# A state-space scan on one core: one state's input of each chunk made by VectorE in place of GpSimd, its row of B broadcast by TensorE

## The chip, the core and the metric

The kernel runs on one core of a Trainium2 chip. The metric is the device time of one execution in microseconds (us). The engines are called PE (TensorE; PEld is its loading of weights), DVE (VectorE), ACT (ScalarE), POOL (GpSimd) and SP (SyncE, which here issues the DMAs). Each has its own instruction queue, works through it in order, and waits for the others by semaphores.

## The reference, cut to what matters

For each of 8 images (56 x 56 pixels, 192 channels) a first layer normalises, runs separable convolutions and attention, and adds the result. A second layer projects to 384 channels, convolves, and runs a selective scan over the 3136 pixels in four directions, 16 states each:

```python
def step(h, inp):
    u_l, d_l, B_l, C_l = inp
    dA = jnp.exp(d_l[..., None] * A)
    dBu = d_l[..., None] * B_l[:, :, None, :] * u_l[..., None]
    h = dA * h + dBu
    y = jnp.sum(h * C_l[:, :, None, :], axis=-1)
    return (h, y)
```

`d` and `u` have a value for every pixel and channel, `B` and `C` one for every pixel and state. The outputs `y` of the four directions are added, normalised, gated and projected. The change concerns `dBu`: the product of `d*u` (made earlier, `du`) with the row of `B` that belongs to one state.

## The kernel before, in words

The scan works in chunks of T = 448 pixels: 7 chunks by 4 directions by 8 images are 224 chunks, and in each chunk 16 states follow one another. The 384 channels lie as NJ = 3 blocks of 128 partitions. For one state `n` of a chunk this happens:

- `row_loads` (line 1098 on) has SP load the row of `B` from DRAM onto all 128 partitions, the tile `bb` (five buffers; 224 KB written to SBUF).
- `inputs_made` (line 1113 on) takes one of seven buffers `h` and has POOL multiply `du` with `bb` into it, 128 x 1344 elements (line 1119).
- `decays` has ACT make the factors exp(d*A), one block at a time, into one of two PSUM banks `da` (line 1133).
- `scans` has DVE run the recurrence along the pixels, in place in `h`, block by block (line 1150); `carries` keeps the last column (line 1172).
- For most states TensorE transposes `h` in four pieces of 112 pixels into the PSUM tile `ht` (`turned`, line 1196), ACT scales it by `C`, which is then one number for each partition, into `g` (line 1212; the column of `C` comes from `ct_s`), and TensorE transposes it back and adds it up in the PSUM tile `y` (`back`, line 1230).
- For the states named in `BY_POOL` (2 and 6, 9 and 13; in the last image 2 and 7, 12) POOL multiplies `h` with a broadcast row of `C` and adds two such products (lines 1248 and 1252), and TensorE adds the sum to `y` (line 1267).
- At the end of a chunk DVE adds `y` to the image's sum (`evicted`, three instructions of line 1282 or 1284). There is one `y`, in three PSUM banks.

PSUM has eight banks: three for `y`, two for `da`, and three that are shared. Of the shared ones `ht` may hold up to two and the rest of the kernel ("bank1") one at a time.

While the scan of an image runs, the first layer of the next image is woven in: in its first part convolutions (line 452) and attention (lines 756 and 765), then the projections of its scan (`x_proj`, lines 936 to 956, where POOL also makes `du`, line 920). In its last direction the finished image is normalised, gated and written (`finish`, lines 984 to 1036).

The order of all engines' queues is fixed when the program is built. Each step is a generator that yields engine, assumed cost, what it reads and what it writes; a planner (`Sched`) always gives out the step that could start soonest, less a rank in us. `pace` ties the next image's TensorE time to the progress of the scan: 87% of it is spread over the first three directions, the rest over the fourth. Where the planner sees TensorE idle for long, it puts in small products with zeros (`warm`, line 1363), the fills. `share(name, most)` (line 1311 on) makes a user of the three shared banks; a bank is asked for with `yield`, and comes free when the instruction that reads it out is placed.

The columns of `C` come from `ct_out` (line 889 on): the transposed projection is copied by DVE from PSUM, stored to DRAM, and loaded again by `prepared`, a chunk ahead, as `ct_s`.

Of the kernel before, what the change touches and what calls it, by code (L numbers as in the profile page):

```python
# [18 lines left out]
L = HW * HW  # L19
# [20 lines left out]


BY_POOL = (((2, 7), (12,)), ((2, 6), (9, 13)))
EPS = 1e-5
CAP = 60.0
HBUFS = 7
# [228 lines left out]
def kernel(  # L274
# [198 lines left out]
    def front(b):  # L473
# [308 lines left out]
        with tc.tile_pool(name=f"fw_{b}", bufs=1) as fw, tc.tile_pool(name=f"fi_{b}", bufs=2) as pool:  # L782
# [7 lines left out]
            for i, w in enumerate((wx, wz)):  # L790
# [10 lines left out]
                rows=[dbatch.tile([2 * NST, L], F32, name=f"rows{k}") for k in range(NDIR)],  # L801
                dl=[dbatch.tile([128, NJ, L], F32, name=f"dl{k}") for k in range(NDIR)],
                du=[dbatch.tile([128, NJ, L], F32, name=f"du{k}") for k in range(NDIR)],
                ct=[dbatch.tile([TP, L // TP, NST], F32, name=f"ct{k}") for k in range(NDIR)],
                k_rows={}, k_ct={}, k_dl={}, k_du={})

            tiles, ends = {}, []
# [67 lines left out]
    def x_proj(b, todo):  # L875
# [3 lines left out]
        with tc.tile_pool(name=f"p2_{b}_{todo[0][1]}", bufs=2) as pool:  # L879
# [7 lines left out]
                    inputs[lay, c] = xs  # L887

            def ct_out(pct, lay, c):
                ct = yield p2("ct", [TP, 2, SUB, NST])  # L890
                yield DVE, 0.25, pct.c, ct.c
                nc.vector.tensor_copy(ct.ap, pct.ap[:TP, :].rearrange("p (s k r) -> p k s r", k=2, r=64)[:, :, :, R + NST:NR])
                pct.free()
                for i in range(2):
                    k = lay + 2 * i
                    m["k_ct"][k, c] = Cell()
                    yield from dma(ct.c, [m["k_ct"][k, c]], 2.9, m["ct"][k][:, c * SUB:(c + 1) * SUB], ct.ap[:, i])
                ct.free()
# [150 lines left out]
    for b in range(nb):  # L1049

        for k in (0, 1, 3, 2):
            order = range(NCH) if k < 2 else range(NCH - 1, -1, -1)
            steps += [(b, k, c, i) for i, c in enumerate(order)]
    todo = [(i, n) for i in range(len(steps)) for n in range(NST)]
    by = [BY_POOL[b < nb - 1] for b, *_ in steps]
    by = [{n: (n == g[0], n == g[-1]) for g in groups for n in g} for groups in by]

# [13 lines left out]
    def prepared():  # L1071

        for i, (b, k, c, _) in enumerate(steps):
            yield lambda: b in made and all((k, c) in made[b][s] for s in ("k_ct", "k_rows", "k_dl", "k_du"))
            m = made[b]
            cols = slice(c * T, (c + 1) * T)
            du = yield s2("du_s", [128, NJ, T])
            yield from dma([m["k_du"][k, c]], du.c, 5.5, du.ap, m["du"][k][:, :, cols])
            dl = yield s2("dl_s", [128, NJ, T])
            yield from dma([m["k_dl"][k, c]], dl.c, 5.5, dl.ap, m["dl"][k][:, :, cols])  # L1080
            ct = yield s2("ct_s", [TP, SUB, NST])
            yield from dma([m["k_ct"][k, c]], ct.c, 1.8, ct.ap, m["ct"][k][:, c * SUB:(c + 1) * SUB])
            chunks[i] = (dl, du, ct)

# [13 lines left out]
    def row_loads():  # L1098
        for i, n in todo:
            b, k, c, _ = steps[i]  # L1100
            yield lambda: i in chunks
            m = made[b]
            cols = slice(c * T, (c + 1) * T)
            bb = yield s3("bb", [128, T], 5)
            yield from dma([m["k_rows"][k, c]], bb.c, 3.2, bb.ap, m["rows"][k][n, cols].partition_broadcast(128))
            brow[i, n] = bb
            if n in by[i]:
                cbr = yield s2("cb", [128, T])
                yield from dma([m["k_rows"][k, c]], cbr.c, 3.2, cbr.ap,
                               m["rows"][k][NST + n, cols].partition_broadcast(128))  # L1110
                crow[i, n] = cbr

    def inputs_made():
        for i, n in todo:
            yield lambda: (i, n) in brow
            bb, du = brow.pop((i, n)), chunks[i][1]
            h = yield sh("h", [128, NJ, T], parts=2 + NJ)
            yield POOL, t_pool(NJ * T), bb.c + du.c, [h.c[0]]
            nc.gpsimd.tensor_tensor(h.ap, du.ap, bb.ap.unsqueeze(1).to_broadcast([128, NJ, T]), ALU.mult)  # L1119
            bb.free()  # L1120
            if n == NST - 1:
                du.free()
            states[i, n] = [h, 2]

    def decays():
        for i, n in todo:
# [75 lines left out]
    def scaled():  # L1202
        for i, n in todo:
            if n in by[i]:
                continue
            for s in range(SUB):
                yield lambda: (i, n, s) in turns
                ct = chunks[i][2]
                ht = turns.pop((i, n, s))
                g = yield s3("g", [TP, DIN])  # L1210
                yield ACT, 0.47, ht.c + ct.c, g.c
                nc.scalar.activation(g.ap, ht.ap[:TP, :DIN], AF.Copy, scale=ct.ap[:, s, n:n + 1])  # L1212
                ht.free()
                gs[i, n, s] = g
            if n == NST - 1:
                ct.free()
# [72 lines left out]
    with tc.manual_schedule():  # L1289
# [11 lines left out]
        with ExitStack() as es:  # L1301
            py = es.enter_context(tc.tile_pool(name="py", bufs=1, space=PSUM))
            pa = es.enter_context(tc.tile_pool(name="pa", bufs=2, space=PSUM))
            pb = [es.enter_context(tc.tile_pool(name=f"pb{i}", bufs=1, space=PSUM)) for i in range(3)]
            ybanks = py.tile([128, NJ, 512], F32, name="y")
            nc.vector.memset(ybanks, 0.0)
            ry = Ring(lambda: ybanks, 1)
            rda = Ring(lambda: pa.tile([128, 512], F32, name="da"), 2)
            three = [Tile(1) for _ in pb]

            def share(name, most):
                return Share(three, [lambda p=p: p.tile([128, 512], F32, name=name, tag="bank") for p in pb], most)

            rht = share("ht", 2)
            banks[0] = share("bank1", 1)
            at["chunk"] = 0
            for g, rank in ((prepared, 0.3), (skips, 0.0), (row_loads, 0.25), (inputs_made, 0.0), (decays, 0.37),
                            (scans, 0.16), (carries, 0.36), (turned, 0.37), (scaled, 0.38), (by_pool, 0.39),
                            (back, 0.4), (summed, 0.0), (evicted, 0.71)):
                sc.spawn(g(), rank, "scan")  # L1320

            per = NDIR * NCH * NST

            def ended(b):
                first = b * NDIR * NCH + (NDIR - 1) * NCH
                yield lambda: at["chunk"] >= first
                yield from finish(b, lambda c: lambda: at["chunk"] >= first + NCH - c, yread[b])

            def arounds():
                for b in range(nb):  # L1330
                    yread[b] = {}
                    sc.spawn(ended(b), 0.0, "finish")
                    if b > 0:
                        yield lambda: at["chunk"] >= b * NDIR * NCH
                    else:
                        yield from sc.join([sc.spawn(x_proj(0, order[LEAD:]), 0.0, "front")])
                    if b + 1 < nb:
                        yield from sc.join([sc.spawn(front(b + 1), 0.0, "front")])
                        yield from sc.join([sc.spawn(x_proj(b + 1, order), 0.0, "front")])

            def pace():

                b, slot = divmod(at["scan"], per)
                whole = main + len(order) * each
                lead = each * (len(order) - LEAD)
                before = b * whole + (lead if b else 0.0)
                here = whole + (0.0 if b else lead)
                late, share = (NDIR - 1) * NCH * NST, 0.87
                part = share * slot / late if slot < late else share + (1.0 - share) * (slot - late) / (per - 2 * NST - late)
                want = before + here * part  # L1350
                return want + 12.0, want - 12.0

            def ending():
                done = sum(len(r) for r in yread.values())
                b, c = divmod(at["chunk"], NDIR * NCH)
                come = b * NCH + max(c - (NDIR - 1) * NCH, 0)
                return 1e9, 1e9 if done < come - 1 or done < b * NCH else 0.0

            def warm():

                while True:
                    yield PE, T_FILL, [], []
                    nc.tensor.matmul(ybanks[:, 0, T:T + FILL], zeros, zeros[:, :FILL], start=False, stop=False)  # L1363

            def may():
                y = ys.get(at["y"])
                return y is not None and y["left"][0] > 0 and y["on"]

            at["y"] = -1
            filler = Stage(warm(), 0.0, 0.0, None)  # L1370
            sc.resume(filler)
            sc.filler = filler, may
            sc.limit["front"] = pace
            sc.limit["finish"] = ending
            sc.spawn(arounds(), 0.0)
            sc.run()
# [58 lines left out]
```

## Time and profile before

| | us |
|---|---|
| median of three runs | 18205.7 (18203.6 to 18205.72) |
| the profiled execution, its own time | 18215.8 |
| its span, first to last instruction | 18214.1 |
| evictions of the fifth image end | 9741 to 11950 |
| evictions of the last image end | 16366 to 18167 |

The span is cut into stretches in some views. A busy time is the sum over an engine's records in the stretch, with the number of instructions behind it; records of PE, DVE and ACT overlap in part, since an instruction starts while the one before it is still draining. A group's row gives line, engine, operation, what it writes and reads, shapes, number, then busy time and mean ns of one, then the idle time of the engine just before these instructions and what ended most of it. A wait's row says who waited for whom, and gives total us, number of waits and the longest.

The chain of work that ended last is followed in this profile only from 16093 us to the end, so it tells of the last image alone, which the change leaves as it is. The mean granted clock of TensorE is 0.982.

### The profile page before, as it was taken

What the parts mean: (1) busy time and instruction counts of PE and PEld (TensorE: products, weight loads), DVE (VectorE), ACT (ScalarE), POOL (GpSimd) and SP (SyncE); (2) the same over time, 40 slices, a digit from 0 to 9 for tenths busy, and PEclk for the clock granted to TensorE, in tenths of its full rate; (3) what the DMA queues carried; (4) which work ended last, traced back from release to release, by engine and by line L of the source; (5) the groups of instructions that cost most, each with busy time, mean ns of one, the idle gap of its engine ahead of it and who ended that gap; (6) DMA issues with size and microseconds to landing.
All of it is one profiled execution on the core that took longest, in us unless ns stands there. A gap on an engine that the chain in (4) does not pass through costs nothing. (4 is left out here: it accounts for less than half of the span.)

```text
span 18214.1 us, 279960 instructions
## 1 busy us (share of the span) xinstructions
PE 16706.4 (92%) x99872; PEld 11743.7 (64%) x99872; DVE 14151.5 (78%) x17811; ACT 14223.5 (78%) x25030; POOL 15560.9 (85%) x5200
## 2 busy tenths in 40 slices
PE   8799999999999999999999999999999999999998
PEld 4466666666666666666666666666666666667776
DVE  2277777788878788787887877878878788888998
ACT  2377788687877878778787887878888787888888
POOL 0288899888998889888898889988899888999998
PEclk9899999999999999999999999999999999999999
DMA  1353345433453334533344334553345433453332
GB/s 54 115 161 90 94 142 158 119 90 107 140 170 97 94 112 139 163 99 95 116 147 152 99 92 120 150 150 95 96 127 155 135 93 95 135 153 120 97 96 78
DMA packets 1363539, 2158.99 MB, mean 119 GB/s; under 512 B 176112, under 2 KB 1346016, under 8 KB 1359072
## 3 DMA queue, kind: packets, MB, share of 16 engines
q1 hardware_dynamic: 1362144, 2141.09, 39.7%
q8 instruction: 791, 12.96, 0.3%
q14 instruction: 604, 4.95, 0.1%
HBM read 1649.41 MB, written 491.21 MB: 118 GB/s over the span
## 5 line engine op out<-in xcount | busy, mean ns | idle before, releaser
L1150 DVE TENSOR_TENSOR_SCAN h<-da,newc,h 128x448 f32<-128x448 f32 x9216 | 10104.9, 1137 | 1970.7 <-ACT da L1133 1380.5
L1119 POOL TENSOR_TENSOR h<-du_s,bb 128x1344 f32<-128x1344 f32 x3584 | 10825.3, 3053 | 927.5 <-PE ht L1196 816.2
L1133 ACT ACTIVATE da<-dl_s,acoef 128x448 f32<-128x448 f32 x10752 | 6750.8, 638 | 1756.9 <-DVE h L1150 1705.7
L1212 ACT ACTIVATE g<-ht,ct_s 112x384 f32<-112x384 f32 x10864 | 5847.5, 575 | 936.1 <-PE ht L1196 771.3
L1230 PEld LDWEIGHTS y<-ident,g 112*128 112x128 f32 x32592 | 3564.4, 142 | 2902.0 <-ACT g L1212 1954.4
L1230 PE MATMUL y<-ident,g 112*128 112x112 f32 x32592 | 4799.3, 268 | 654.3 <-ACT g L1212 530.1
L1196 PE MATMUL ht<-ident,h 128*112 128x128 f32 x32592 | 4944.2, 276 | 122.5 <-ACT g L1212 46.6
L1196 PEld LDWEIGHTS ht<-ident,h 128*112 128x112 f32 x32592 | 3683.2, 135 | 482.7 <-DVE h L1150 147.3
L1150 DVE TENSOR_TENSOR_SCAN h<-da,h 128x448 f32<-128x448 f32 x1536 | 1607.5, 1078 | 459.6 <-ACT da L1133 410.9
L1248 POOL TENSOR_TENSOR yp<-h,cb 128x1344 f32<-128x1344 f32 x448 | 1366.3, 3050 | 407.6 <-PE y L1267 173.7
L1248 POOL TENSOR_TENSOR h<-h,cb 128x1344 f32<-128x1344 f32 x420 | 1281.6, 3051 | 292.0 <-issue 171.9
L1363 PE MATMUL y<-zeros 128*128 128x64 f32 x11648 | 1486.5, 271 | 0.0
L1363 PEld LDWEIGHTS y<-zeros 128*128 128x128 f32 x11648 | 1444.5, 194 | 50.2 <-issue 50.2
L920 POOL TENSOR_TENSOR v<-v,xs 128x1344 f32<-128x1344 f32 x224 | 677.3, 3043 | 824.7 <-DMA dl<-v 773.6
L1252 POOL TENSOR_TENSOR yp<-yp,h 128x1344 f32<-128x1344 f32 x420 | 1280.1, 3048 | 32.2
L452 PE MATMUL bank<-xa,dg 128*128 128x440 f32 (+2 forms) x3024 | 1237.1, 535 | 24.2 <-ACT xv L824 19.2
L1267 PE MATMUL y<-yp,ident 128*128 128x448 f32 x2688 | 1223.4, 546 | 10.7 <-POOL yp L1252 10.2
L756 PE MATMUL bank<-qT,kT 128*112 128x448 f32 x2352 | 1074.5, 573 | 138.6 <-DVE oT L719 82.9
L765 PE MATMUL bank<-pT,vt 112*128 112x448 f32 x2352 | 999.9, 543 | 12.4 <-ACT g L1212 6.6
L706 ACT ACTIVATE pT<-bank,nsh 112x448 f32<-112x448 f32 x1176 | 740.1, 632 | 207.2 <-PE bank L756 167.1
L452 PE MATMUL bank<-band,dgq 96*96 96x440 f32 (+3 forms) x2016 | 806.4, 532 | 10.7 <-ACT hq L582 7.7
L452 PEld LDWEIGHTS bank<-xa,dg 128*128 128x128 f32 x3024 | 525.8, 191 | 364.6 <-issue 289.9
(146 smaller groups left out, 11082.0 us busy)
## 6 DMA issues: line engine op xcount, KB each, us to landing
bb<-rows SPq DMA_DIRECT2D x3584, 224.0 KB, 3.4
cb<-rows SPq DMA_DIRECT2D x868, 224.0 KB, 3.7
dl<-v SPq DMA_DIRECT2D x224, 672.0 KB, 5.0
du<-v SPq DMA_DIRECT2D x224, 672.0 KB, 6.1
du_s<-du SPq DMA_DIRECT2D x224, 672.0 KB, 4.5
dl_s<-dl SPq DMA_DIRECT2D x224, 672.0 KB, 4.6
xt<-x1d SPq DMA_DIRECT2D x224, 336.0 KB, 4.6
xch<-xv SPq DMA_DIRECT2D x24, 1568.0 KB, 7.3
```

What stands on the lines that cost most here:

```text
L452: nc.tensor.matmul(out[:, o0:o1, a:b], lhs, img(lo, hi)[:, :, a + dx - 1:b + dx - 1], start=(t == TAPS[0]), stop=(t == TAPS[-1]))
L756: nc.tensor.matmul(ps.ap[:TP, :T], kts[h][:, kb * TP:(kb + 1) * TP], qh.ap, start=True, stop=True)
L1119: nc.gpsimd.tensor_tensor(h.ap, du.ap, bb.ap.unsqueeze(1).to_broadcast([128, NJ, T]), ALU.mult)
L1133: nc.scalar.activation(da.ap[:, :T], dl.ap[:, j], AF.Exp, scale=acoef[:, k * NJ + j, n:n + 1])
L1150: nc.vector.tensor_tensor_scan(h.ap[:, j, rev], da.ap[:, 0:T][:, rev], h.ap[:, j, rev], news[i - 1].ap[:, j, n:n + 1] if ci else 0.0, ALU. ...
L1196: nc.tensor.transpose(ht.ap[:TP, j * 128:(j + 1) * 128], h.ap[:, j, s * TP:(s + 1) * TP], ident)
L1212: nc.scalar.activation(g.ap, ht.ap[:TP, :DIN], AF.Copy, scale=ct.ap[:, s, n:n + 1])
L1230: nc.tensor.matmul(y["t"].ap[:, j, s * TP:(s + 1) * TP], g.ap[:, j * 128:(j + 1) * 128], ident[:TP, :TP], is_transpose=True, start=(n == 0 ...
L1248: nc.gpsimd.tensor_tensor(to.ap, h.ap, cbr.ap.unsqueeze(1).to_broadcast([128, NJ, T]), ALU.mult)
L1252: nc.gpsimd.tensor_tensor(yp.ap, yp.ap, h.ap, ALU.add)
L1267: nc.tensor.matmul(y["t"].ap[:, j, :T], ident, yp.ap[:, j], start=False, stop=(y["left"][j] == 0))
L1363: nc.tensor.matmul(ybanks[:, 0, T:T + FILL], zeros, zeros[:, :FILL], start=False, stop=False)
```

## The change

For state 7 of every chunk of the first seven images the load of `bb` and POOL's product go. In their place TensorE transposes the column of `B` of that state, read 128 times over, in four pieces of 112 pixels into one PSUM bank (`bc`): each of the 128 partitions then holds the row. DVE multiplies `du` with it into `h`. For this the columns of `B` have to be in `ct_s` beside those of `C`, so that the tiles and copies of `ct` become twice as wide. `bc` is a further user of the three shared banks and may hold one.

```diff
 BY_POOL = (((2, 7), (12,)), ((2, 6), (9, 13)))
+BY_DVE = ((), (7,))
...
-                ct=[dbatch.tile([TP, L // TP, NST], F32, name=f"ct{k}") for k in range(NDIR)],
+                ct=[dbatch.tile([TP, L // TP, 2 * NST], F32, name=f"ct{k}") for k in range(NDIR)],
...
             def ct_out(pct, lay, c):
-                ct = yield p2("ct", [TP, 2, SUB, NST])
-                yield DVE, 0.25, pct.c, ct.c
-                nc.vector.tensor_copy(ct.ap, pct.ap[:TP, :].rearrange("p (s k r) -> p k s r", k=2, r=64)[:, :, :, R + NST:NR])
+                ct = yield p2("ct", [TP, 2, SUB, 2 * NST])
+                yield DVE, 0.35, pct.c, ct.c
+                nc.vector.tensor_copy(ct.ap, pct.ap[:TP, :].rearrange("p (s k r) -> p k s r", k=2, r=64)[:, :, :, R:NR])
...
+    by_dve = [BY_DVE[b < nb - 1] for b, *_ in steps]
...
-            ct = yield s2("ct_s", [TP, SUB, NST])
+            ct = yield s2("ct_s", [TP, SUB, 2 * NST])
...
-            bb = yield s3("bb", [128, T], 5)
-            yield from dma([m["k_rows"][k, c]], bb.c, 3.2, bb.ap, m["rows"][k][n, cols].partition_broadcast(128))
-            brow[i, n] = bb
+            if n in by_dve[i]:
+                brow[i, n] = None
+            else:
+                bb = yield s3("bb", [128, T], 5)
+                yield from dma([m["k_rows"][k, c]], bb.c, 3.2, bb.ap, m["rows"][k][n, cols].partition_broadcast(128))
+                brow[i, n] = bb
...
             h = yield sh("h", [128, NJ, T], parts=2 + NJ)
+            if n in by_dve[i]:
+                sc.spawn(input_made(i, n, h), 0.1)
+                continue
...
+    def input_made(i, n, h):
+        _, du, ct = chunks[i]
+        bc = yield rbc
+        yield PE, 0.41, ct.c, bc.c
+        for s in range(SUB):
+            nc.tensor.transpose(bc.ap[:, s * TP:(s + 1) * TP], ct.ap[:, s, n:n + 1].to_broadcast([TP, 128]),
+                                ident[:TP, :TP])
+        yield DVE, 1.45, bc.c + du.c, [h.c[0]]
+        nc.vector.tensor_tensor(h.ap, du.ap, bc.ap[:, :T].unsqueeze(1).to_broadcast([128, NJ, T]), ALU.mult)
+        bc.free()
+        states[i, n] = [h, 2]
...
-                nc.scalar.activation(g.ap, ht.ap[:TP, :DIN], AF.Copy, scale=ct.ap[:, s, n:n + 1])
+                nc.scalar.activation(g.ap, ht.ap[:TP, :DIN], AF.Copy, scale=ct.ap[:, s, NST + n:NST + n + 1])
...
-            rht = share("ht", 2)
+            rht, rbc = share("ht", 2), share("bc", 1)
```

`BY_DVE[b < nb - 1]` is `(7,)` for the first seven images and empty for the last one.

## The prediction, made before the changed kernel ran

> **What bounds the kernel now.** I read the engines' busy shares first, then the granted clock, then the stretches of one image, then the waits inside two of them. The page's first line of busy times puts no engine at its limit over the whole span:
>
> ```profile
> PE 16706.4 (92%) x99872; PEld 11743.7 (64%) x99872; DVE 14151.5 (78%) x17811; ACT 14223.5 (78%) x25030; POOL 15560.9 (85%) x5200
> ```
>
> PE's 92% is no 92% of its capacity: the records overlap (a 268 ns record of line 1230 is followed by the next 96 ns later, in the timeline), and 1486 us of it are the fills of line 1363, which stand only where PE would be idle. POOL's records hardly overlap: in the timeline one 3.05 us operation follows another after 3.00 us. So POOL, at 85% in all, is the fullest engine, and the question is where it is full.
>
> I cut the fifth image (9741 to 11950 us) at the ends of its evictions (lines 1282 and 1284, three for each chunk): chunks 1 and 2, 3 to 15, 16 to 20, 21 to 28. The fifth row is from the last image. Columns: stretch, length, busy time and instructions of PE, PEld, DVE, ACT, POOL, granted clock, DMA share, GB/s.
>
> ```profile
> 9741.00:9975.00 234.00, 212.34 (x1286) 155.57 (x1284) 154.42 (x217) 150.03 (x241) 167.76 (x61) 0.96 0.53 167
> 9975.00:10957.00 982.00, 903.81 (x5295) 618.05 (x5295) 809.77 (x1001) 798.65 (x1475) 870.99 (x289) 0.99 0.34 95
> 10957.00:11323.00 366.00, 345.64 (x1965) 236.16 (x1965) 293.67 (x359) 296.14 (x520) 328.35 (x109) 1.00 0.42 121
> 11323.00:11950.00 627.00, 577.77 (x3601) 417.42 (x3601) 511.48 (x645) 526.40 (x878) 600.26 (x201) 0.99 0.50 149
> 16600.00:17600.00 1000.00, 921.54 (x7209) 758.41 (x7208) 913.96 (x1104) 875.94 (x1647) 995.83 (x332) 1.00 0.34 97
> ```
>
> The same stretches for the fills of line 1363 alone (PE and PEld):
>
> ```profile
> 9975.00:10957.00 982.00, 34.17 (x242) 32.44 (x242) 0.99 0.34 95
> ...
> 11323.00:11950.00 627.00, 75.34 (x604) 74.05 (x604) 0.99 0.50 149
> ```
>
> I call the four stretches A, B, C and D. In D POOL is busy 600 of 627 us (96%), PE has 604 fills, and DVE and ACT stand at 82 and 84%: POOL is the limit. In B POOL is at 89% and PE has 242 fills in a stretch half as long again; the next image's attention and convolutions fill PE there. The waits say the same. Columns: total us, times, longest. The first two rows are of B, the other two of D:
>
> ```profile
> POOL h L1119 <- PE ht L1196: 51.9, 22, 5.5
> DVE h L1150 <- POOL h L1119: 19.2, 9, 8.7
> ```
> ```profile
> DVE h L1150 <- POOL h L1119: 8.5, 7, 2.2
> POOL h L1119 <- PE ht L1196: 6.7, 2, 4.1
> ```
>
> In B POOL waits 52 us for TensorE to turn a state and so free one of the seven `h` buffers: POOL is ahead there. In D it almost never waits (6.7 us). C is between (90%); A has 66 us of POOL idle in 234. In the last image POOL is at 99.6%, but there the change moves nothing (`BY_DVE[False]` is empty).
>
> **What is removed.** 7 images x 28 chunks = 196 inputs of state 7 leave POOL, and with them 196 loads of `bb`. Prices, each row with mean ns after the busy time:
>
> ```profile
> L1119 POOL TENSOR_TENSOR h<-du_s,bb 128x1344 f32<-128x1344 f32 x3584 | 10825.3, 3053 | 927.5 <-PE ht L1196 816.2
> ...
> L1230 PEld LDWEIGHTS y<-ident,g 112*128 112x128 f32 x32592 | 3564.4, 142 | 2902.0 <-ACT g L1212 1954.4
> L1230 PE MATMUL y<-ident,g 112*128 112x112 f32 x32592 | 4799.3, 268 | 654.3 <-ACT g L1212 530.1
> ...
> L986 DVE TENSOR_TENSOR yacc<-yacc,bank 128x1344 f32<-128x1344 f32 x56 | 86.3, 1540 | 18.0 <-PE bank L984 18.0
> ```
>
> POOL loses 196 x 3.053 = 598 us, 3.05 a chunk. That is the ceiling of any gain, and it is paid only where POOL is late. The 196 loads cost nothing now but for the 39.3 us that POOL waited for `bb` in all (the wait view of line 1119); 1 of 16 of that is 2 us, which I drop. SP's queue loses the same 196 issues, which wait there for POOL to free a `bb` buffer; what follows them on SP can only come sooner.
>
> **What is added.**
> - TensorE: four transposes a chunk. The nearest row is line 1230, also 112 rows of weights and 112 moving columns, 96 ns from start to start in the timeline; with the gap to other work (four of line 945, 128 columns wide, take 438 ns to the next start) I take 0.43 us. A column read 128 times over as weights stands in no row: if it hides nothing, load and matmul follow one another, 4 x (142 + 268) = 1.64 us; at the least it is free, where a fill gives way. I stay with 0.43, the like row.
> - VectorE: one product of 1344 elements with one operand in PSUM, put on three blocks. Line 986 is that very form: 1540 ns busy, 1.44 us to the next start. Ends: 1.44, and 2.66 us, the pitch where something waited. I take 1.5. Behind it wait the scans of line 1150; for them ACT, which has only two `da` banks, and behind ACT the products `g` and TensorE. In D DVE idles 116 of 627 us, so 8 x 1.5 = 12 us are covered; in B it idles 172 of 982 for 19 us. If that cover fails, it is 1.5 us a chunk.
> - The PSUM bank: `bc` becomes the fourth user of three banks, of which `ht` may hold two and the front one. It is held through 0.43 us of transposes, about one scan in front on DVE (1.1) and the product (1.5): 3.1 us. Meanwhile `ht` or the front has one bank less. With one bank a turn and its scaling follow one another: three transposes (0.33), 0.58 us of ACT and some 0.2 between, 1.1 us, where B has a turn each 1.57 us (982 us by 624 scalings). So it would mostly still keep up. Ends: 0 and the whole hold, 3.1. I take 0.2 a chunk in A, B and C, nothing in D, where the fills show that PE has room.
> - Small things, at nothing: the copy of `ct` doubles from 128 to 256 columns. 286 ns becomes about 416 (by the 609 ns of the 448-column copy at line 591, an estimate), 112 x 0.13 = 15 us of DVE in the whole kernel, under DVE's idle time, 15 us if not. The `ct` DMAs carry twice the bytes, land in a median of 2.1 us, and are a chunk ahead. DVE takes the product in its own queue, so state 7 no longer waits for POOL.
>
> **A rule against it.** The last image is the row: of its 7209 PE instructions in 1000 us all but the 1876 fills and the sums of line 1267 are transposes, and the granted clock is 1.00. The Trainium skill, "TensorE: Matmul & The Clock Gate", Part 4 (PE-mode transpose), holds that transposes do not count for the clock gate as ordinary matmuls do; it also gives a gated clock of half speed. An estimate by that page: 4 x 96 ns would be 0.77 us, 75 us more over 196 chunks if nothing covers it. This case's clock, with 65,000 transposes in it, does not agree, and I leave it out.
>
> **The sum for one image.**
> - A, 2 chunks: POOL's time is worth nothing, PE +0.43, bank +0.2: +1.3 us.
> - B, 13 chunks: the same: 13 x 0.63 = +8.2.
> - C, 5 chunks: 5 x 3.05 = 15.3 us leave POOL, which idles a tenth; I count a third, -5.1, and +3.2 for PE and bank: -1.9.
> - D, 8 chunks: 24.4 us leave POOL, which idles 27; I count eight tenths, -19.5. What is late next is the ring between the `da` exponentials and the scans (waits of 56 and 54 us in D).
>
> Together -11.9 us, times 7 images -83 us (the first image, whose start differs, is taken as the others). The profiled execution took 18215.8 us (span 18214.1), so 18133 for it; the median of the three runs is 10 us lower, 18205.7, which gives **18120 us** (-0.5%). This forecast's own range is 18010 to 18190: D worth five to ten tenths (12 to 24 us), C 0 to 10, PE and bank 4 to 14 us.
>
> **Rivals.**
> - *POOL is the limit in more of the image.* For it: it is the fullest engine in every stretch, and DVE waits for its `h` in all four. Against it: it waits 52 us in B for buffers. Were C and half of B POOL's as well, 8 + 5 + 6 chunks x 3.05 x 0.9 = -52 us, +7 for PE and bank in the rest: -45 an image, 17890.
> - *Nothing changes.* The 3.05 us turn into idle time of POOL in D too, since the scans wait there for `da` (56 us) rather than for POOL (8.5): D and C worth 9 us together, against 9.5 + 3: some +3 an image, 18225. This holds too if the product is put so late on DVE that the scan of state 7 waits as before: the change then doesn't relieve what it means to.
> - *Slower: the bank.* In A, B and C the front holds its one bank nearly always; `bc` leaves `ht` a single one for 3.1 us, three turns lose 0.55 us each (1.1 against ACT's own 0.58), 1.65 us a chunk. 20 x (0.43 + 1.65) = 42 us, less 19.5 in D: +22 an image, +155: 18360. It decides from about 0.8 us a chunk on, where 20 x (0.43 + 0.8) equals the 24.6 us of C and D.
>
> **How the numbers follow.** Chances: the forecast 0.48, POOL further 0.14, nothing 0.16, the bank 0.22. What a measurement of this kernel tells from no change is about 0.2%, 36 us. The forecast lies beyond that but for 0.02: faster 0.60, same 0.18, slower 0.22. Range: from 17950, which leaves out the better part of the first rival, to 18300, which takes in "nothing" and half of the bank.
>
> **What would show it.** In the changed profile line 1119 has 3388 instructions, the new DVE product 196 of about 1.54 us, PE 784 transposes more. D of the fifth image lasts about 608 us, with POOL at 95% or less; B some 990. Waits of `ht` or of the front's bank for the new DVE product, over 0.8 us a chunk, would show the bank rival; POOL waiting more in D by what it lost, with D as long as before, the second; B shorter by 10 us or more, the first. The prediction is wrong above all if B isn't PE's, or if the three banks are the tightest thing in it.

## The result, and the profile after

The changed kernel takes 18455.4 us (median of four runs, 18454.1 to 18460.3) against 18205.7 us of the kernel before, measured beside it: a ratio of 1.0138, 95% interval 1.012 to 1.0155. It is slower by 250 us. The forecast was 18120, and the time lies beyond the upper end of its range, 18300.

The busy line of the page after, for the one shown of before:

```profile
PE 16845.7 (91%) x100648; PEld 11845.6 (64%) x100648; DVE 14427.0 (78%) x18007; ACT 14247.7 (77%) x25030; POOL 14973.1 (81%) x5004
```

The work moved as announced: GpSimd has 196 instructions less, VectorE 196 more, TensorE 776 more (784 transposes, 8 fills less). POOL lost 588 us of busy time, and the kernel became longer. Now the groups of what was moved and added (mean ns of one after the busy time):

```profile
L1127 POOL TENSOR_TENSOR h<-du_s,bb 128x1344 f32<-128x1344 f32 x3388 | 10232.2, 3051 | 919.0 <-PE ht L1216 786.7
...
L1141 DVE TENSOR_TENSOR h<-du_s,bc 128x1344 f32<-128x1344 f32 x196 | 302.8, 1545 | 60.3 <-PE bc L1138 60.3
L1138 PE MATMUL bc<-ident,ct_s 112*128 112x112 f32 x784 | 110.1, 263 | 0.7 <-ACT g L1232 0.2
```

The prices of the single instructions were right: 1545 ns against 1540 for the product, and in the timeline the transposes follow one another every 96 ns. So the loss is not in what the instructions cost but in where they stand. The four stretches of the fifth image in the kernel after, cut at the same evictions as before:

```profile
9860.00:10124.00 264.00, 233.63 (x1377) 169.98 (x1376) 168.53 (x237) 160.67 (x258) 174.54 (x63) 0.95 0.52 163
10124.00:11119.00 995.00, 916.48 (x5314) 626.07 (x5311) 817.46 (x1002) 797.31 (x1470) 825.03 (x274) 0.98 0.33 91
11119.00:11495.00 376.00, 353.31 (x2007) 242.04 (x2008) 308.98 (x374) 301.30 (x528) 318.78 (x106) 1.00 0.37 115
11495.00:12104.00 609.00, 561.28 (x3560) 406.41 (x3558) 512.68 (x636) 515.47 (x860) 564.94 (x189) 1.00 0.48 146
```

A is 264 us in place of 234, B 995 in place of 982, C 376 in place of 366, D 609 in place of 627. D came out as forecast (608), B near it (990); C went the wrong way, and A, where I had counted 1.3 us, took 30 more. The fills in B and D stand nearly as before:

```profile
10124.00:11119.00 995.00, 34.35 (x234) 32.61 (x234) 0.98 0.33 91
...
11495.00:12104.00 609.00, 73.94 (x584) 71.99 (x584) 1.00 0.48 146
```

The waits that were shown for B (two rows) and D (two rows) are now these; POOL waits for buffers as much as before, though it has less to do:

```profile
POOL h L1127 <- PE ht L1216: 59.9, 21, 7.5
...
DVE h L1170 <- POOL h L1127: 14.5, 9, 5.1
```
```profile
POOL h L1127 <- PE ht L1216: 4.5, 2, 2.5
DVE h L1170 <- POOL h L1127: 4.3, 1, 4.3
```

What did grow over the whole span is ScalarE's wait for a turned state, from 771 to 1070 us (before, line 1212; after, line 1232):

```profile
L1212 ACT ACTIVATE g<-ht,ct_s 112x384 f32<-112x384 f32 x10864 | 5847.5, 575 | 936.1 <-PE ht L1196 771.3
```
```profile
L1232 ACT ACTIVATE g<-ht,ct_s 112x384 f32<-112x384 f32 x10864 | 5869.6, 575 | 1279.7 <-PE ht L1216 1070.1
```

The turned states lie in the shared banks, so the bank was the first suspect; the 30 us at the start of each image were the second. The sign that the prediction named for the bank did not come: TensorE and its loads wait some 31.5 us in all for the new product (the view of the tile `bc`, eight rows), 0.16 us a chunk in place of 0.8. The two largest rows:

```profile
PEld ht L1216 <- DVE h L1141: 16.5, 44, 0.8
...
PE ht L1216 <- DVE h L1141: 6.5, 14, 0.6
```

One more view matters for what follows: what TensorE does for the front (the next image's first layer and projections, and the finished image's last steps), which all goes through the tile `bank`. Stretches A and D of the fifth image, before and after (PE, PEld, DVE, ACT, then clock and DMA as above):

```profile
9741.00:9975.00 234.00, 102.73 (x408) 57.17 (x406) 34.10 (x59) 8.85 (x19) 0.96 0.53 167
...
11323.00:11950.00 627.00, 196.28 (x588) 91.74 (x588) 76.90 (x115) 19.81 (x37) 0.99 0.50 149
```
```profile
9860.00:10124.00 264.00, 118.80 (x453) 65.52 (x451) 40.48 (x69) 10.54 (x22) 0.95 0.52 163
...
11495.00:12104.00 609.00, 183.94 (x553) 85.15 (x552) 73.34 (x106) 17.46 (x33) 1.00 0.48 146
```

D has 35 such instructions less after the change, and A 45 more: the two stretches no longer hold the same work.

### The profile page after: what moved, and what is told of

It reads as the page before. It is cut to its first block, busy times and chain, and to the rows that moved or that the text cites. A ratio compares the mean times of both kernels' runs of the same rounds, so it can differ in the third digit from the quotient of the medians.

```text
span 18453.0 us, 280923 instructions
## 1 busy us (share of the span) xinstructions
PE 16845.7 (91%) x100648; PEld 11845.6 (64%) x100648; DVE 14427.0 (78%) x18007; ACT 14247.7 (77%) x25030; POOL 14973.1 (81%) x5004
## 5 line engine op out<-in xcount | busy, mean ns | idle before, releaser
L1127 POOL TENSOR_TENSOR h<-du_s,bb 128x1344 f32<-128x1344 f32 x3388 | 10232.2, 3051 | 919.0 <-PE ht L1216 786.7
```

## The experiments

All times are compared with the kernel before, measured beside them (its median lay between 18207.6 and 18221.8 us). A to D are means over the third to seventh image of the profiled execution, cut at the evictions. "Left over" is the number of pieces of the next image's projections (14 in an image, each begun by one copy `xd` on ScalarE) that start only after the image's last eviction, for these five images.

| kernel | us | minus before | ratio, 95% interval | A | B | C | D | left over |
|---|---|---|---|---|---|---|---|---|
| before | 18205.7 | | | 233 | 982 | 367 | 626 | 3 |
| after | 18455.4 | +250 | 1.0138 (1.012 to 1.0155) | 263 | 997 | 375 | 610 | 4 |
| e1 three directions | 18484.6 | +270 | 1.0143 (1.0128 to 1.0158) | 247 | 1007 | 375 | 623 | 3 |
| e2 last direction | 18325.2 | +110 | 1.0060 (1.0045 to 1.0075) | 260 | 977 | 367 | 620 | 4 |
| e3 row by DMA | 18592.3 | +377 | 1.0205 (1.0188 to 1.0222) | 232 | 997 | 384 | 647 | 2 or 3 |
| e4 no product | 18157.3 | -58 | 0.9967 (0.9954 to 0.998) | 224 | 981 | 366 | 628 | 2 |
| e5 bank alone | 18426.9 | +207 | 1.0113 (1.0098 to 1.0128) | 225 | 1009 | 369 | 632 | 2 |
| e6 VectorE alone | 18326.1 | +106 | 1.0058 (1.0043 to 1.0073) | 230 | 999 | 367 | 627 | 2 or 3 |
| e7 null order | 18216.5 | -4 | 1.0001 (0.9992 to 1.0011) | 236 | 978 | 367 | 629 | 2 |
| e8 after, rank 0.3 | 18452.4 | +232 | 1.0128 (1.0113 to 1.0143) | 264 | 985 | 367 | 627 | 4 |
| e9 TensorE alone | 18124.1 | -98 | 0.9950 (0.9935 to 0.9964) | 243 | 967 | 369 | 616 | 3 |
| e10 bank without TensorE | 18238.6 | +17 | 1.0011 (1.0001 to 1.002) | 247 | 977 | 367 | 614 | 2 or 4 |
| e12 state not turned | 18002.8 | -219 | 0.9879 (0.9863 to 0.9896) | 233 | 966 | 359 | 623 | 2 or 3 |
| e15 last image relieved | 18199.7 | -22 | 0.9989 (0.998 to 0.9999) | 226 | 982 | 368 | 632 | 2 or 3 |
| f1 = e8, pace 0.90 | 18374.3 | +164 | 1.0092 (1.0077 to 1.0107) | 223 | 1014 | 352 | 639 | 1 or 2 |
| f2 = before, pace 0.90 | 18246.3 | +36 | 1.0017 (1.0008 to 1.0027) | 222 | 996 | 349 | 642 | 1 |
| f3 = after, pace 0.90 | 18407.2 | +197 | 1.0110 (1.0095 to 1.0125) | 227 | 1022 | 356 | 634 | 2 |
| f4 = e5, rank 0.3 | 18316.0 | +106 | 1.0059 (1.0044 to 1.0074) | 261 | 980 | 361 | 614 | 4 |
| f5 four states relieved | 18615.7 | +408 | 1.0224 (1.0209 to 1.0239) | 254 | 999 | 364 | 624 | 4 |
| f6 null order 2 | 18199.9 | -8 | 0.9997 (0.9987 to 1.0007) | 232 | 982 | 366 | 626 | 3 |

My theory after the result was "handed back": the gain in D is real, but the start of the next image pays for projections that no longer fit into the shorter D. Its rivals were "bank" (the fourth user of the shared banks), "product" (VectorE's 1.5 us) and "order" (luck of the planner).

### Which directions lose

```diff
-    by_dve = [BY_DVE[b < nb - 1] for b, *_ in steps]
+    by_dve = [BY_DVE[b < nb - 1 and k != 2] for b, k, *_ in steps]
```

> State 7 goes to VectorE only in the first three directions of an image (21 of 28 chunks); the last direction is as before. Theory 'handed back': the changed kernel gains 18 us an image in stretch D and the start of the next image (A) loses 29, because work of the next image's projections is left over when D is shorter. Then here D and A are as before (627 and 234 us), only B and C stay longer (13 + 9 us): about 18205 + 7 x 22 = 18360. Theory 'bank': the fourth user of three banks costs time wherever bc is used, so A stays near 263 us and B and C long: 18205 + 7 x 50 = 18550.

Measured: +270, more than the whole change. D is nearly as before (623), but A is 247, and B 1007. Neither theory had it: A is longer by 14 us although D isn't shorter by much, and it isn't at 263 either.

```diff
-    by_dve = [BY_DVE[b < nb - 1] for b, *_ in steps]
+    by_dve = [BY_DVE[b < nb - 1 and k == 2] for b, k, *_ in steps]
```

> The other half: state 7 goes to VectorE only in the last direction (7 of 28 chunks). 'Handed back': D some 15 us shorter, A of the next image longer by as much or more, 0 to +11 us an image: 18200 to 18290. 'Bank': D shorter, A as before: 18205 - 7 x 15 = 18100.

Measured: +110, above both theories. D gains 6 us and A loses 27, with nothing of the change in A. So A pays for something that is done in D: the part of "handed back" that places the loss stands, though D gained far less than A lost. The two halves together (+380) are more than the whole: the parts don't add.

### The product without the bank

```diff
-        bc = yield rbc
-        yield PE, 0.41, ct.c, bc.c
-        for s in range(SUB):
-            nc.tensor.transpose(...)
         yield DVE, 1.45, bc.c + du.c, [h.c[0]]
-        nc.vector.tensor_tensor(h.ap, du.ap, bc.ap[:, :T]..., ALU.mult)
+        nc.vector.tensor_tensor(h.ap, du.ap, bb.ap..., ALU.mult)
...
```

The row of `B` is loaded into `bb` for state 7 too, as in the kernel before.

> VectorE still makes the product of state 7, but reads the row of B from bb, loaded by DMA as before: no transposes, no bc, no fourth user of the shared banks. 'Bank': B and C lose nothing and A little: 18100 to 18200. 'Product' (the 1.5 us of VectorE in front of the scan of state 7 are what costs, whatever feeds it): as the changed kernel, 18400 to 18460. 'Handed back' alone says nothing of B and C, but keeps A at 250 us or more.

Measured: +377, the slowest but one, and no theory had it. The group's row gives the likely reason; the same product with both operands in SBUF takes 3475 ns in place of 1545:

```profile
L1133 DVE TENSOR_TENSOR h<-du_s,bb 128x1344 f32<-128x1344 f32 x196 | 681.0, 3475 | 1.8 <-PE ht L1208 1.5 <-issue 0.3
```

The 1.93 us more, 196 times, are 378 us, about the loss; how much of them is exposed was not measured, and that the two sums agree so closely is no proof. So this run says nothing of the bank. It is told under the hardware below.

### Relief alone

```diff
-                sc.spawn(input_made(i, n, h), 0.1)
+                h.c[0].w = max(du.c[0].w, h.c[0].r)
+                states[i, n] = [h, 2]
...
+                src = chunks[i][1] if n in by_dve[i] else h
...
                 nc.vector.tensor_tensor_scan(
-                    h.ap[:, j, rev], da.ap[:, 0:T][:, rev], h.ap[:, j, rev],
+                    h.ap[:, j, rev], da.ap[:, 0:T][:, rev], src.ap[:, j, rev],
```

> State 7's input is not made at all in the first seven images: its scan takes du itself (the factor B is left out), so GpSimd is relieved and nothing is put on VectorE, TensorE or the banks. 'Handed back': D about 20 us shorter, A longer by 15 to 25: 18150 to 18250, which would show that relief of GpSimd is worth little in this program whoever does the work. 'Bank' and 'product': nothing is added, so the relief is kept: 18205 - 7 x 20 = 18065 or less.

Measured: -58 us, 0.3 us of each 3.05 us that GpSimd no longer does. This is the run that fells the forecast. D of the fifth image in e4:

```profile
11284.00:11913.00 629.00, 580.07 (x3591) 420.21 (x3591) 510.36 (x640) 527.22 (x875) 574.27 (x191) 0.99 0.49 149
```

POOL is busy 574 us in place of 600 (the 25 us are gone, as worked out), and D is as long as before. POOL was 96% busy there and was not the limit. "Handed back" falls in its first half too: there was no gain in D to hand back.

The same in the last image, where POOL was at 99.6%:

```diff
-BY_DVE = ((), (7,))
+BY_DVE = ((7,), ())
```

> As e4, but the product of state 7 is left out in the last image and made as before in the other seven: 28 chunks in place of 196. There GpSimd is busy 99.6% and waits for nothing, in D of the others 96%. If only the first is a limit: 28 x 2 to 3 us = 56 to 84 us less, 18120 to 18150, as much as e4 gets from 196 chunks. If relief of GpSimd is worth e4's 0.3 us a chunk there too: 18197 or more.

Measured: -22 us. The stretch 16700 to 17600 us of before and of e15:

```profile
16700.00:17600.00 900.00, 830.13 (x6491) 683.05 (x6490) 822.17 (x994) 789.39 (x1484) 895.99 (x299) 1.00 0.34 97
```
```profile
16700.00:17600.00 900.00, 829.63 (x6495) 682.77 (x6493) 822.52 (x994) 790.21 (x1484) 849.13 (x282) 1.00 0.34 93
```

POOL falls from 99.6% to 94%, and the other engines do in these 900 us what they did before, nearly to the instruction (VectorE 994 and 994, ScalarE 1484 and 1484). A chunk takes 60.6 us before and 60.7 in e15, from eviction to eviction. In both kernels the scans of successive states start mostly 3.82 us apart, and 3.32 us apart two states behind those that POOL multiplies. The work of VectorE and of ScalarE comes near to that: three scans of 1.067 us and a carry of 0.08 are 3.28 us; three `da` of 0.56 and four `g` of 0.46 are 3.52 (starts in the timeline). Neither fills 3.82 us alone, and what makes up the rest was not isolated. GpSimd's 20 operations of 3.0 us a chunk need as long, and it works up to seven states ahead: it is always busy, and with one operation less the chunk is no shorter.

### VectorE, TensorE and the bank, one at a time

All four leave the product out like e4, and add one part again.

VectorE's time without bank and TensorE (a sum over `du` whose result isn't used):

```diff
-        nc.vector.tensor_tensor(h.ap, du.ap, bc.ap..., ALU.mult)
+        nc.vector.tensor_reduce(few.ap, du.ap.rearrange("p j t -> p (j t)"), AX.X, ALU.add)
```

> As e4, but VectorE sums du over its 1344 columns (one input, about 1.45 us, the result unused) ahead of the scan of state 7: VectorE's time without transposes and bank. 'Product': 18350 to 18455, 196 x 1.5 = 294 us over e4, every microsecond of it exposed. 'Bank': 18157 to 18220. 'Order': anywhere between.

Measured: +106, so 164 us over e4, of 284 us (196 x 1.45) that were added. It is in B: 999 against 981 us, 1.4 us for each of 13 chunks, nearly the whole 1.45. C and D hide it.

TensorE's transposes into spare columns of `ht`:

```diff
                 for j in range(NJ):
                     nc.tensor.transpose(ht.ap[:TP, j * 128:(j + 1) * 128], ...)
+                if n in by_dve[i]:
+                    nc.tensor.transpose(ht.ap[:, DIN:DIN + TP], <column n of ct, 128 times>, ident[:TP, :TP])
```

> As e4 (no product; state 7 scans du), plus TensorE's four transposes a chunk written to spare columns of the ht tiles that are held anyway: TensorE's 0.4 us a chunk without a bank and without a wait of VectorE. e4 took 18157, e5 (transposes and bank) 18427. 'TensorE's time': 0.4 to 0.5 us x 196 = 80 to 100 us at the most, 18240 to 18260. 'Bank': the rest, so that this run stays at 18157 to 18260, far from 18427.

Measured: -98, 40 us below e4, with more work. TensorE's time costs nothing that can be seen; that the 40 us are the planner's other order is likely, but not shown.

The bank without transposes:

```diff
         bc = yield rbc
-        yield PE, 0.41, ct.c, bc.c
-        <four transposes>
-        yield DVE, 1.45, bc.c + du.c, [h.c[0]]
-        nc.vector.tensor_tensor(h.ap, du.ap, bc.ap..., ALU.mult)
+        yield DVE, 0.08, [], [h.c[0]] + bc.c
+        nc.vector.memset(bc.ap[:, 0:1], 0.0)
```

> As e5, but nothing is transposed: a shared bank is taken for bc, VectorE writes one column of it (0.08 us), the scan waits for that, and the bank is given back. 'Bank': most of the 270 us between e4 and e5 are here, 18300 to 18427, although the hold is short. 'TensorE': near e4, 18157 to 18200. If neither e9 nor this one comes near 18427, it is the joint hold: the bank is kept while the transposes wait for their turn on TensorE.

Measured: +17, 75 us over e4, short of what "bank" expected. B and C are as in e4 or better. The 75 us lie in A, and only in some images: the third and fourth, with 2 pieces left over, have A at 222 us and the D before it at 621; the fifth to seventh, with 4, have 263 and 614. One program shows both, so A follows how much is left over, and not what the program adds to a chunk: A and the D before it together are 844 us with 2 and 877 with 4.

Transposes and bank together, no product:

```diff
-        yield DVE, 1.45, bc.c + du.c, [h.c[0]]
-        nc.vector.tensor_tensor(h.ap, du.ap, bc.ap..., ALU.mult)
+        yield DVE, 0.08, bc.c, [h.c[0]] + few.c
+        nc.vector.tensor_copy(few.ap, bc.ap[:, 0:1])
```

> As e4 (state 7 scans du, no product, B left out there), but the four transposes into bc are made and the scan waits for one column of bc that VectorE copies (0.08 us). That is TensorE's part and the bank, without the 1.5 us of VectorE. e4 took 18157 us, the changed kernel 18455: 298 us to divide. 'Bank': 18350 to 18455. 'Product': 18157 to 18200. 'Order' (any change of the planner's order moves the time by some hundred us): anywhere between 18100 and 18450, with nothing that points to the bank.

Measured: +207, 265 us over e4, as "bank" had it. B is 1009 us against 981: 2.2 us a chunk with hardly any work added. Together they cost what neither costs alone (e9, e10), and B holds the same work of the next image in e4 and e5 (1146 and 1150 instructions of `bank` on TensorE). So I looked at how long the bank is held, from the first transpose to the end of the read that frees it, from their records: 7.0 us on average here and 6.7 in the changed kernel, where I had worked out 3.1. The average hides the place: in B it is 5.2 us here and 6.5 in the changed kernel, whose B is shorter, and in A it is 21.9 us here, though A is as short as in e4 (225 and 224). So the length of the hold does not set the price by itself. One such hold in the timeline of the changed kernel, chunk 11 of the fifth image (start, length, engine, line):

```profile
10732.91 2.19 DVE L1170 TENSOR_TENSOR_SCAN h<-da,newc,h 128x448 f32<-128x448 f32 x2 [0.51 <-ACT da L1153]
10733.57 0.55 PE L1138 MATMUL bc<-ident,ct_s 112*128 112x112 f32 x4
10735.13 0.16 DVE L1192 TENSOR_REDUCE newc<-h 128x3 f32<-128x3 f32 x1
...
10740.43 3.23 DVE L1170 TENSOR_TENSOR_SCAN h<-da,newc,h 128x448 f32<-128x448 f32 x3
10743.70 0.16 DVE L1192 TENSOR_REDUCE newc<-h 128x3 f32<-128x3 f32 x1
10743.78 1.55 DVE L1141 TENSOR_TENSOR h<-du_s,bc 128x1344 f32<-128x1344 f32 x1
10745.44 2.19 DVE L1170 TENSOR_TENSOR_SCAN h<-da,newc,h 128x448 f32<-128x448 f32 x2
```

The row lies ready in `bc` at 10734.1. VectorE does two more states first, and makes the product right ahead of the scan that needs it (10745.44). The bank is gone for 11.8 us, in which `ht` and the front share two. The waits hardly name this: ScalarE's wait for turned states in B is 76 us an image here as in the changed kernel, where e4 has 49; but e10 has 66 with a short B, so that this wait alone is not the price.

### The length of the hold

```diff
-                sc.spawn(input_made(i, n, h), 0.1)
+                sc.spawn(input_made(i, n, h), 0.3)
```

This in e5:

> e5 (four transposes into bc and one short copy on VectorE, no product; 18427 us) with rank 0.3 in place of 0.1: the copy is placed sooner behind the transposes. In e5 the bank is held 7.0 us on average from the first transpose to the end of the copy; in e8 rank 0.3 brought it to 2.7. 'Hold': B falls from 1009 to about 981 us and the time to 18160 to 18260. If the bank costs by being taken at all, whatever the length: 18380 or more.

Measured: the hold is 1.2 us (1.3 in B), and B falls from 1009 to 980 us, C from 369 to 361. The time falls only to +106, since now 4 pieces are left over and A is 261. Not all of B's 29 us are the hold, since the longer A takes work over from B; `bank` on TensorE in B of the fifth image, e5 and then f4:

```profile
10091.00:11098.00 1007.00, 423.11 (x1151) 169.18 (x1150) 37.31 (x73) 115.42 (x193) 0.98 0.33 91
```
```profile
10054.00:11030.00 976.00, 408.30 (x1100) 162.66 (x1098) 34.05 (x67) 114.97 (x193) 0.98 0.33 92
```

These are 54 instructions less on average over the five images. What that is worth differs: from image to image of one program, 44 less go with 3 us in B (e10), 21 less with 6 us (e6) or 16 us (e3). So part of the fall is the hold, since rank is all that was changed, but how much of it stays open.

This in the changed kernel:

> The changed kernel with rank 0.3 in place of 0.1 for the new steps: the same work, the new product is placed a little sooner. 'Order': moves by 90 us or more. 'Bank' and 'product': 18400 to 18500, since the same bank and the same 1.5 us are paid.

Measured: +232, the same as the change, where "bank" and "product" had it. By stretches it isn't the same: the hold is 2.7 us, the product stands ahead of its scan by 9 us in B (median) in place of 3, and B and C are back at 985 and 367, within 3 us of the kernel before, with bank and product in place. The time is lost in A, 264. But A does more there: TensorE has 482 instructions of `bank` in A, 1100 in B and 562 in D, where the kernel before has 406, 1150 and 588. So B and D do less and are no shorter, and what bank and product cost there is hidden by that.

### The start of an image

A goes with the pieces left over in the 13 kernels with pace 0.87 up to here (before, after, e1 to e10, e12): with 2 left (24 images) A is 221 to 239 us, with 3 (23 images) 227 to 250, with 4 (18 images) 259 to 266; A and the D before it together are 857, 863 and 880 on average. Counted in TensorE's instructions of the projections (308 in an image), and over all 17 kernels with this pace, two groups part: with 60 to 70 left for A it takes 221 to 239 us, with 82 to 92 239 to 266. The kernel before leaves 70, the changed one 88. A shorter D goes with more left over on average (629, 626, 618), as it should if D's gain is work put off; e8 is an exception, with 4 left and D at 627. To move the leftovers I changed the pace:

```diff
-                late, share = (NDIR - 1) * NCH * NST, 0.87
+                late, share = (NDIR - 1) * NCH * NST, 0.90
```

In e8:

> e8 (rank 0.3 for the new steps) with the pace's share 0.90 in place of 0.87: more of the next image's TensorE work in the first three directions, so that its projections are further on when the image ends. In e8, B, C and D are as before and A is 263 us in place of 233, with 4 pieces of the projections left over where the kernel before has 3. 'Left over': 2 or 3 are left, A returns to 223 to 240 us: 18452 - 7 x 30 = 18240. 'Not left over, the product itself': A stays, 18400 to 18480.

In the kernel before:

> The kernel before with the share 0.90: the comparison for the two others of this call. 3 pieces are left over with 0.87; with 2 A is some 8 us shorter, but B takes 3% more of the next image's work: 18150 to 18280.

In the changed kernel:

> The changed kernel with the share 0.90. 'Left over' says that A falls from 263 to 225 to 240 us, and that B and C stay longer by the long hold of the bank (13 and 9 us): 18455 - 7 x 27 = 18265. If A stays at 260: 18400 or more.

Measured: 1 or 2 pieces are left over, and A is 222 to 227 us in all three, as "left over" had it. But the time is not won: B takes the work (f2 has 996 us against 982), and the kernel before itself becomes slower by 36 us. At this pace the change costs f1 128 us and f3 161 over f2, where it costs 250 at 0.87. So some 90 us of the 250 hang on the pace and with it on the leftovers, and the rest is mostly in B (f1 +17, f3 +26 an image over f2).

### What another engine's relief is worth

```diff
+LEFT_OUT = ((), (7,))
...
+            if n in left_out[i]:
+                over(i, n)
+                continue
             for s in range(SUB):
                 ht = yield rht
...
```

> The kernel before; state 7 of the first seven images isn't turned, scaled and added to y (its part of the output is left out). TensorE loses 4 x (3 x 0.109 + 3 x 0.096) = 2.5 us a chunk, ScalarE 4 x 0.46 = 1.8, the shared banks 4 turns of 49; GpSimd keeps all. 'GpSimd was never the limit' (what e4 says): it pays far more than e4's 58 us, 196 x 1.5 to 2.5 = 290 to 490: 17730 to 17920. 'All are equally coupled': as little as e4, 18100 to 18180.

Measured: -219, less than I expected, but nearly four times e4's 58, for 2.5 us of TensorE and 1.8 of ScalarE a chunk (as worked out above) where e4 takes 3.05 from GpSimd. The path through TensorE, the shared banks and ScalarE is nearer to the limit than GpSimd; which of the three it is, this run doesn't tell.

### Order alone, and four products

```diff
-                            (inputs_made, 0.0)
+                            (inputs_made, 0.05)
```

> The kernel before with the rank of inputs_made 0.05 in place of 0.0: the same instructions with the same work, in another order wherever two steps were close. 'Order': the time moves by 0.5% or more (90 us) one way or the other, and no difference below that can be put down to a cost. 'Bank' and 'product': within 0.2%, 18180 to 18250.

```diff
-            (row_loads, 0.25) ... (scaled, 0.38)
+            (row_loads, 0.2) ... (scaled, 0.41)
```

> The kernel before with two ranks changed (row_loads 0.20 in place of 0.25, scaled 0.41 in place of 0.38): a second kernel with the same work in another order, beside e7 (18217). It gives how far the time moves by order alone: within 40 us if e7 was typical, with 2 or 3 pieces left over at the image's end; near 18300 to 18400 if the order happens to leave 4.

Measured: -4 and -8 us. The queues differ from the kernel before in thousands of places, and the time doesn't move. So a changed order need not cost anything, and "order" as a shift that any change brings is out. It is not out for A: what decides how much is left over is the planner's order, and no run here settles it.

```diff
-BY_DVE = ((), (7,))
+BY_DVE = ((3, 7, 11, 14), (3, 7, 11, 14))
```

This in e4:

> e4 four times over and in all eight images: the products of states 3, 7, 11 and 14 are left out (their scans take du), 12.2 us of GpSimd less in every chunk, nothing added. 'GpSimd was near the limit in D and the rest hides it after one product': D stays at 620 to 630 us as in e4, with GpSimd at some 80%, and all seven images lose about what e4 lost (9 us), so 18150; the last image, where GpSimd was at 99.6%, falls from 60.8 us a chunk to the next engine's limit (VectorE at 0.87 of 60.8, 53 to 56 us), 28 x 5 to 8 = 140 to 220 us: 17930 to 18010 in all. 'GpSimd is a limit everywhere by its queue's length': D falls by 30 us or more an image, 17800 or less.

Measured: +408, though 12 us of GpSimd's work are left out in every chunk. I expected a gain under any theory. A chunk of the last image takes 67.6 us in place of 60.6, and GpSimd is at 71% there:

```profile
16900.00:17800.00 900.00, 833.71 (x6602) 701.96 (x6601) 735.30 (x889) 712.91 (x1331) 642.92 (x213) 1.00 0.25 74
```

The 7 us are lost before two states, 11 and 13, whose scans start 6.7 and 8.4 us after the ones before them in place of 3.9 and 3.8. Why the planner leaves these holes stays open; one guess, not tested, is that buffers `h` taken without a product are held longer. The run shows that relief which the planner spends badly can cost, and it limits e4: "relief alone" is a price in this planner's order, not a pure one.

No kernel that computes the whole reference came out below the kernel before by more than its interval.

## Why the prediction was wrong, point by point

- **"In D POOL is ... the limit", and "D, 8 chunks: ... I count eight tenths, -19.5": the step that failed.** Taking the 25 us from POOL leaves D at 628 us (e4). I took a high busy share, and few waits of POOL itself, for a limit. Both are also what an engine shows that works ahead and has about as much to do as the stretch is long, as GpSimd in the last image (e15). What spoke against it stood in the same fence: VectorE waited for POOL 8.5 us in D. Even 99.6% there was no limit. I had this as the reason of the second rival, and gave it 0.16.
- **That D came out at 609, as forecast, is a hit for a wrong reason.** D holds less of the front's work (552 TensorE instructions on average in place of 588, where e4 has 593 and the old length), and A does more (449 in place of 406). e10 shows the same within one program: 593 and 621 us in one image's D, 558 and 614 in the others'. In A + D the forecast had -18.2 us and the runs +13.2. Not every kernel fits: in e8 D has 562 and is as long as before, and what it pays for was not isolated.
- **"A, 2 chunks: ... +1.3 us": measured +29.5.** The step assumed that A does its own work alone. It begins with what the image before left over; 4 pieces in place of 3 are 25 us in A on average over the 13 kernels (262 and 238). This term alone is 28 of the 47 us an image by which the sum was off (C 10, B 6, D 3). No row of the forecast looked across the end of an image. What decides between 2 and 4 I could not settle: bank or product are in most kernels with 4, but f5 has neither, and e5, with a hold of 7.0 us, has 2.
- **VectorE's product.** Its price was right (1.5), its cover was not: "in B it idles 172 of 982 for 19 us" holds as arithmetic, but e6 pays 18 us in B, all of it. So the idle time there was no free room for it. Placed 9 us ahead of its scan (e8) the product costs B 3 us with the bank included, but with 50 instructions of the next image less in B, so that its price there stays open.
- **The bank.** "It is held through ... 3.1 us": 6.7 us. I added up the instructions and forgot that the planner may make the read last, as it does (38% of the products in B and 80% in C stand directly ahead of their scan). The price of 0.2 us a chunk was as wrong: 2.2 us a chunk in B in e5. The third rival had the nearest mechanism, with 1.65 us a chunk, 18360 and a chance of 0.22. Its own sign, waits for the new product of over 0.8 us a chunk, came to 0.16, and it missed A, where most of the loss lies.
- **TensorE's 0.43 us and the small things.** The transposes follow one another as priced, but the sum counted them as time lost, and by e9 they cost nothing. The copy of `ct` takes 416 ns on average, as estimated.
- **"+8.2" for B** came out at +14.4, C at +7.9 in place of -1.9. Without anything added, C gains 2 us by GpSimd's relief (e4), where I had counted 5; in the changed kernel C also holds 414 TensorE instructions of the front in place of 400.
- **The clock** stayed at 0.982, as argued against the Trainium skill, "TensorE: Matmul & The Clock Gate", Part 4 (PE-mode transpose). The fills don't explain it alone: in the kernel before, from 2723.5 us on, the trace shows nothing on TensorE but 135 transposes for 19.2 us (lines 1196 and 1230), at a granted clock of 1.00.

The sum as measured, for each of the third to seventh images: A +29.5, B +14.4, C +7.9, D -16.3, together +35.5, where the forecast had -11.9. The parts don't add up over the experiments: e6 and e5 cost 164 and 265 us over e4, the change with both 308. So it is shown that GpSimd's relief was worth little, and that a held bank with its transposes (e5) and the product (e6) each cost time in B. That A's 30 us are work left over fits all runs with this pace; why so much is left over stays open.

## What to carry to other kernels

Busy 96 or 99.6% is not yet a limit: ask who waits for that engine, and if hardly anyone does, take a piece of its work out in a test before moving the work elsewhere. Price a shared buffer by the time from its first write to the placed end of its last read, not by the instructions in between, and see where the planner puts that read; here even that did not give the price alone. A stretch that became shorter may have put work off: compare the sum of two neighbouring stretches, and count what each of them does.

## What the runs showed of the hardware

A VectorE product of 128 x 1344 took 1545 ns with one operand in PSUM (after, line 1141), and 3475 ns on average, up to 11.6 us, with both in SBUF (e3, line 1133), beside the same GpSimd work. The 25 of e3's products that overlapped no GpSimd operation took 1543 ns. The 99 that took over 2.5 us all end 1.41 to 1.42 us after the end of a GpSimd operation: it looks as if VectorE stood still until GpSimd was through, sometimes through several in a row. GpSimd suffers less, 3072 ns on average over all its products against 3053; but the 43 operations that began beside a product over 2.5 us and outlasted it took 4.2 us (median). The Trainium skill, "SBUF — State Buffer", section "Who interferes with whom", says so: a VectorE instruction with two SBUF inputs contends with a GpSimd instruction that reads SBUF, one with a single SBUF input doesn't. These rows agree on both halves. It is a reason for bringing the row of `B` through PSUM, and that takes a bank.
